# Graph convolutions of a GNN and FFN kernel: the last three or four target tiles summed from gathered rows by rank, the edge table made for 22 target tiles

## The chip, the cores and the metric

The kernel runs on one core of a Trainium2 chip. The metric is the device time of one execution in microseconds, as the median over several runs. The engines are called by the profile's names: PE (TensorE), DVE (VectorE), ACT (ScalarE), POOL (GpSimd) and SP (SyncE, which only issues DMAs). PEld is PE's loading of weights.

## The reference

A graph of 3125 nodes with 256 features and 50000 directed edges, sorted by their target, goes through four pairs of a graph layer and a feed-forward layer, all in FP32. Each adds to `x` and reads a layernorm of it:

```python
x = x + L0_gnn(layernorm(x))    # graph attention, 4 heads
x = x + L0_ffn(layernorm(x))    # 8 experts, top 2
x = x + L1_gnn(layernorm(x))    # two graph attention layers
x = x + L1_ffn(layernorm(x))    # an LSTM over the nodes
x = x + L2_gnn(layernorm(x))    # three graph convolutions
x = x + L2_ffn(layernorm(x))    # 8 experts, top 2
x = x + L3_gnn(layernorm(x))    # one graph convolution
x = x + L3_ffn(layernorm(x))    # 8 experts, top 2
```

What the change touches is the graph convolutions. A layer of the third block is

```python
# src, dst hold the edges and a self loop for each node; norm = disq[src] * disq[dst]
h = h @ W
msg = h[src] * norm[:, None]
h = segment_sum(msg, dst, num_segments=n) + b      # relu between layers
```

with `disq` the inverse square root of a node's number of incoming edges. The fourth block's single layer is the same without self loops and bias.

## The kernel before

**Tiles and stages.** Nodes stand in 25 tiles of 128 (`NT`), the last one with 53 real nodes. `x` stays in SBUF. The stages follow one another: first attention (`gnn0`), experts f0, second and third attention (`gnn1`), the LSTM (`recurrence`: a projection, then rounds), the three convolutions g2 (`gcn`), experts f2, the convolution g3 (`gcn`), experts f3.

**The edge table.** A convolution sums, for each target node, the rows of its sources. The kernel does that as matmuls with a table `ctm` of edge counts, sources by targets, in bf16. `table` (L640) makes it during the first attention in 200 windows of 16 targets: DVE compares keys (L662, L672), PE makes three matmuls for each window (L681), ACT casts them (L688), SP stores them. Between windows, `ahead` (L1224) issues a share of the gathered attention, whose edges POOL fetches by indirect DMA (L2023) and which the later sweep over tiles finishes; `apart.share` rises to 0.55 over the windows.

**Two convolutions, transposed.** `convolve` (L1529) walks over spans of four or three target tiles. For each it loads the table's columns by `table_columns` (L814; five source tiles to a DMA, three buffers) and, over 25 source tiles, makes 2 x 3 matmuls (two halves of the features, three bf16 parts of the FP32 rows `hs`), into `acc0` and `acc1` with two buffers each. `done` scales them on DVE (L1663), applies bias and relu on ACT (L1664), multiplies by the next layer's weights on PE (L369), scales on ACT into `new` (L1656), and `parted` (L840) splits `new` into three bf16 parts, on POOL (casts L847, L849) and DVE (L848, L850). Self loops are an identity that POOL adds to the loaded columns (L828).

**Two convolutions by rows.** `convolve_rows` (L1546), the last layer of g2 and the one of g3, walks over spans of two target tiles with the table as stationary operand (L1560: two parts, 512 wide; L1564: the third, 256 wide); DVE adds the scaled sums to `x` (L1684). After each span, `ready` hands pieces of the expert routing (`experts.front`: norms, router, scatter of rows by L2348) to later steps of the loop, by lags in steps of one target tile and source tile. Weight loads for the experts are spread over the same steps.

**What sets the order.** Each engine runs its own list of instructions in order. The lists come from the order in which the program records instructions and from the scheduler of the framework, which places them by its own estimate of time. `issue_after(ins)` orders only what is on the engine of `ins`. DMA queues take transfers in order of issue: SP for table columns and weights, ACT for stored rows, POOL for gathers and scatters.

**Experts.** `load_ahead` (L2400) loads, once the table's last columns are on the queue, row units (`load_rows`) and first weights (`load_first`, 1158 KB each for f2); f2 has `early=6, ahead=2, more=3`.

**Projection.** In `recurrence` (L1801 to L1824) 98 steps each make 16 matmuls into `px`, four PSUM buffers, which DVE adds to the bias into `pre`.

**Flags.** Numbers in `flags` that are not zero at the end start a second, general computation (L2816 on), which doesn't use the early assumptions.

## Time and profile before

| quantity | value |
|---|---|
| median of 3 runs | 4117.46 us (4089.36 to 4130.27) |
| the profiled execution | 4123.68 us, span 4121.8 us, mean granted TensorE clock 0.913 |
| busy share of the span | PE 86%, PEld 52%, DVE 52%, POOL 34%, ACT 29% |
| table windows (first to last cast) | 94.7 to 437.7 us |
| LSTM projection | 1759.4 to 1826.2 us |
| g2, two transposed convolutions | 2539.1 to 2761.5 and 2761.5 to 2984.0 us |
| g2, convolution by rows | 2984 to about 3200 us |
| f2 experts | about 3240 to 3607 us |
| g3, projection and convolution | about 3607 to 3900 us |
| f3 experts | about 3900 to 4121 us |
| DMA | 422.32 MB, mean 102 GB/s |

The times of stages are from the span's start. A group of instructions in the profile has its line, engine, operation, tiles, count, busy time, mean duration in ns, and the idle time of its engine just before, with what released it. Matmuls overlap: a duration of 379 ns can go with a spacing of 220 ns, so spacings are taken from the timeline. Idle time of an engine that is not the bottleneck costs nothing.

### The profile page before, as it was taken

To read this page: it belongs to the slowest core of one execution; us is meant where nothing else is said; L and a number is where in the kernel's file an instruction comes from. 1 tells how busy PE (TensorE), PEld (TensorE's weight loads), DVE (VectorE), ACT (ScalarE), POOL (GpSimd) and SP (SyncE) were. 2 spreads that over 40 slices of the span, in tenths; PEclk is the share of its full clock that TensorE was granted. 3 is DMA by queue.
4 is the path that set the end of the run, shared out by engine and by line. 5 is a ranking of instruction groups with operands and counts; after the bars stand their busy time and mean duration, and the time that the engine had idled before them with its cause. 6 is when DMAs were issued, how large, how long until landed. Compare 5 with 4: busy or idle time off the path is not lost. (4 is left out here: it accounts for less than half of the span.)

```text
span 4121.8 us, 72442 instructions
## 1 busy us (share of the span) xinstructions
PE 3555.9 (86%) x25990; PEld 2149.1 (52%) x26079; DVE 2155.3 (52%) x7897; ACT 1212.7 (29%) x4041; POOL 1401.9 (34%) x1321
## 2 busy tenths in 40 slices
PE   4567878676878868899999998999999999989988
PEld 3233222463222356675454455555566788856677
DVE  7567788646766645557677675111156411153411
ACT  2455333434333302114444444000100322330122
POOL 2756666444767357400000003111122222222243
PEclk8666887798989979999999999999999999989999
DMA  4444432563333254300000002333364444445465
GB/s 123 136 137 143 141 105 79 142 223 109 107 105 108 73 156 140 87 3 2 2 2 2 2 2 61 88 94 92 91 197 143 144 117 117 122 129 157 134 158 122
DMA packets 366387, 422.32 MB, mean 102 GB/s; under 512 B 44076, under 2 KB 320864, under 8 KB 362295
## 3 DMA queue, kind: packets, MB, share of 16 engines
q1 hardware_dynamic: 286833, 260.46, 21.0%
q0 software_dynamic: 62224, 140.41, 13.1%
q10 hardware_dynamic: 16950, 16.54, 1.2%
q8 instruction: 219, 3.59, 0.4%
q14 instruction: 161, 1.32, 0.1%
HBM read 337.37 MB, written 82.62 MB: 102 GB/s over the span
## 5 line engine op out<-in xcount | busy, mean ns | idle before, releaser
L2023 POOL DMA_INDIRECT edge<-scored,from x720 | 830.6, 1154 | 517.9 <-issue 238.9
L1540 PE MATMUL acc<-c,hs 128*128 128x512 bf16 (+1 forms) x2069 | 405.9, 356 | 1.7 <-POOL hs L847 0.2
L1801 PE MATMUL pz<-lstm_v,hist 128*32 128x192 f32 x7120 | 382.5, 333 | 19.3 <-DVE hist L1906 7.3
L1560 PE MATMUL acc<-hs,c 128*128 128x512 bf16 x1192 | 394.9, 379 | 0.0
L2689 PE MATMUL ph<-xt,first 128*128 128x256 f32 (+1 forms) x1624 | 351.1, 371 | 5.7 <-ACT xt L2655 3.1
L1564 PE MATMUL acc<-hs,c 128*128 128x256 bf16 x1250 | 340.6, 272 | 3.0
L2707 PE MATMUL py<-w,ht 128*128 x1484 | 337.8, 382 | 4.5 <-issue 4.1
L2082 ACT ACTIVATE edge<-edge,factor 128x65 f32<-128x65 f32 (+1 forms) x960 | 251.3, 349 | 218.8 <-DVE factor L2077 170.4
L2689 PEld LDWEIGHTS ph<-xt,first 128*128 128x128 f32 x1624 | 290.6, 196 | 41.3 <-ACT xt L2655 5.4
L1540 PEld LDWEIGHTS <-hs 128*128 128x128 bf16 x2100 | 205.6, 98 | 199.2 <-POOL hs L847 0.6
L2707 PEld LDWEIGHTS py<-w,ht 128*128 128x128 f32 x1484 | 282.9, 192 | 43.6 <-issue 5.2
L976 DVE SCALAR_TENSOR_TENSOR v<-q,g1ahv,c 128x384 f32<-128x384 f32 (+1 forms) x400 | 240.4, 646 | 112.0 <-remote 52.3
L1837 PE MATMUL pz<-pre,ident 128*128 128x192 f32 x900 | 268.4, 381 | 12.1 <-PEq L1914 11.6
L1801 PEld LDWEIGHTS pz<-lstm_v,hist 128*32 128x32 f32 x7120 | 186.0, 109 | 167.7 <-DVE hist L1906 135.9
L2348 POOL DMA_INDIRECT slots<-rows,sloti x150 | 168.5, 1123 | 307.5 <-DVE rstd L345 136.7
L2697 ACT ACTIVATE ht<-ph,first 128x256 f32<-128x256 f32 (+1 forms) x406 | 160.8, 456 | 323.2 <-PE ph L2689 284.3
L681 PE MATMUL pa<-hi,lo 128*128 128x350 bf16 (+2 forms) x600 | 166.4, 422 | 96.8 <-ACT cols L688 40.4
L1611 POOL TENSOR_TENSOR disc<-deg,expo 128x25 f32<-128x25 f32 x1 | 4.4, 4360 | 714.6 <-DVE ends L1911 714.6
L1131 PE MATMUL acc<-g1bhv,v 128*128 128x257 f32 x850 | 218.0, 407 | 25.2 <-issue 9.9
L1884 ACT ACTIVATE z<-pz 128x128 f32<-128x128 f32 (+1 forms) x900 | 176.5, 248 | 198.1 <-PE pz L1801 197.5
L2092 PE MATMUL edgeacc<-edge,hot 128*32 128x264 f32 (+1 forms) x1440 | 152.3, 468 | 82.2 <-issue 35.1
L1837 PEld LDWEIGHTS pz<-pre,ident 128*128 128x128 f32 x900 | 136.0, 190 | 149.0 <-issue 70.3
(530 smaller groups left out, 5499.2 us busy)
## 6 DMA issues: line engine op xcount, KB each, us to landing
c<-ct SPq DMA_DIRECT2D x103, 640.0 KB
c<-ct SPq DMA_DIRECT2D x75, 480.0 KB
first<-in_f_first SPq DMA_DIRECT2D x29, 1158.0 KB
slots<-slots SPq DMA_DIRECT2D x159, 130.0 KB
ct<-cols SPq DMA_DIRECT2D x12, 1600.0 KB
first<-in_f_first SPq DMA_DIRECT2D x29, 642.0 KB
edge<-scored,from POOLq DMA_INDIRECT x720
first<-in_f_first SPq DMA_DIRECT2D x29, 385.0 KB
```

The source lines that it names most:

```text
L976: nc.vector.scalar_tensor_tensor(to, q[:, h, :w], hv[:, s, h, D // nh + 1 : D // nh + 2], cols[s], op0=ALU.max, op1=ALU.mult,)
L1131: nc.tensor.matmul(a[:, : D + 1], v[0][:, j * P : (j + 1) * P], hv[:, s, 0, : D + 1], start=(s == 0), stop=(s == NT - 1),)
L1540: self.nc.tensor.matmul(acc[f][:, : n * P], lhs, cols[s], start=(s == 0 and i == 0), stop=(s == NT - 1), skip_group_check=True,)
L1560: nc.tensor.matmul(acc[t], lhs, hs[:, s, 0:2, :].rearrange("p i d -> p (i d)"), start=start, stop=stop, skip_group_check=True,)
L1564: return nc.tensor.matmul(acc[t][:, D:], lhs, hs[:, s, 2, :], start=False, stop=stop, skip_group_check=True,)
L1801: made = nc.tensor.matmul(pz[q * R : (q + 1) * R, :], s, m, start=start, stop=stop, tile_position=(0, q * R),)
L1837: made = nc.tensor.matmul(pz, self.ident, pre[:, g, s, :], start=True, stop=False)
L1884: nc.scalar.activation(three[0][:, gates, :], three[1][:, gates, :], AF.Tanh)
L2023: nc.gpsimd.indirect_dma_start(out=tile[:, g, :], out_offset=None, in_=self.rows, in_offset=bass.IndirectOffsetOnAxis(ap=index, axis=0),)
L2082: nc.scalar.mul(part, part, factor[:, g, h : h + 1])
L2689: made = nc.tensor.matmul(ph[:, m - m0, :n, :], st["w1"][:, k * hid + m * P : k * hid + (m + 1) * P], st["xt"][:, k, :n, :], start=(k == 0 ...
L2707: nc.tensor.matmul(py[:, j, :], st["ht"][:, m, j, :], st["w2"][:, m * D : (m + 1) * D], start=(m == 0), stop=(m == nhc - 1),)
```

## The change

**Near tiles.** With `NEAR = 4`, `RANKS = 22` and `FAR = NT - NEAR = 21`, the last four target tiles (21 to 24) of the transposed convolutions, and the last three (22 to 24) of those by rows, get no matmuls with the table. `NearTiles` sums their sources by rank instead: the r-th incoming edge of each of 128 targets is fetched as one indirect gather of 128 rows from a DRAM copy of the layer's rows (`sources`, written by `put_rows` on ACT's queue), two gathers to a buffer `got`, five buffers; DVE adds them, 128x512 at a time. Edges beyond rank 22 are fetched by one more gather (`more`, at most 128 rows) and spread by a matmul with `beyond_hot`. The end of a near tile is one or two further adds, the scale, and in the transposed layers two transposes, relu and the next product. The recording goes by a clock of 0.325 us for each target tile and source tile.

**The plan.** `near_plan`, 15 pieces recorded after every fourth step of the LSTM projection, works out the indices: degrees, offsets by prefix sums (`before`, two matmuls and a scan on DVE), four gathers of windows of the sorted edges (`win`), five shifts by binary digits (`shifted`, three DVE instructions each), the ranks, the leftovers and one gather of their pairs. Two flags are added: more than 128 leftovers, and a rank whose target doesn't fit.

**The rest.** The table is made for 22 tiles of targets, 176 windows; the gathered attention's share beside it is 0.52. Spans of the transposed convolutions are 4, 3, 4, 3, 4, 3 tiles instead of 4, 4, 3, 4, 3, 4, 3, those of the rows eleven of two instead of twelve and one of one. The routing of the near tiles is taken up after targets 12 and 18. The weights of `gcn` stand in a pool that ends before the rows; in g3 their load comes ahead of the loads of `x` on SP's queue. Experts that store load four row units ahead (f2 two before), f2 one first weight ahead (two before), and `run` loads all early row units at its start into a pool of their own.

```diff
+NEAR, RANKS = 4, 22
+FAR = NT - NEAR
...
+        self.sources = [dram.tile([NP + P, D], F32, name=f"sources{i}") for i in range(2)]
...
+        def where():
+            before(indeg, NT, off)
+            nc.vector.tensor_copy(at, off)
+            nc.vector.tensor_scalar(
+                row, at, RUN.bit_length() - 1, None, op0=ALU.logical_shift_right
+            )
+            for i in range(NEAR):
+                nc.gpsimd.indirect_dma_start(
+                    out=win[:, i, :], out_offset=None, in_=self.runs,
+                    in_offset=bass.IndirectOffsetOnAxis(ap=row[:, i : i + 1], axis=0),
+                )
...
+        def shifted(j):
+            step = 2 << j
+            upto_ = size + step - 2
+            now = pairs[:, :, :upto_]
+            nc.vector.tensor_sub(less[:, :, :upto_], pairs[:, :, step : step + upto_], now)
...
+            nc.vector.tensor_add(now, now, less[:, :, :upto_])
...
-        block, end = 2 * P // WIN, NT * P // WIN
+        block, end = 2 * P // WIN, (FAR + 1) * P // WIN
...
-                        apart.share = 0.55 * (i + 1) / len(windows)
+                        apart.share = 0.52 * (i + 1) / len(windows)
...
-        for t0, n in even_spans(wide):
+        for t0, n in even_spans(wide, FAR if near else NT):
...
-                        self.nc.tensor.matmul(
+                        made = self.nc.tensor.matmul(
...
+                if near:
+                    near.upto(n, made.ins)
...
-        for t0, n in spans(wide):
+        for t0, n in even_spans(wide, near.first if near else NT):
...
+            for other in fronts.pop(t0 + n, ()) if near else ():
+                for lag, piece in ready(*other):
+                    waiting.append((step + 24 + lag, piece))
...
+                def end():
+                    self.put_rows(self.sources[layer % 2], new, t0, n)
+                    self.parted(lefts, to, new, t0, n)
...
+                def near_done(t, rows, i=i, after=after, next_layer=next_layer):
+                    turned, agg = [], aggs.tile([P, KD, P], F32, name="nearagg")
+                    def turn():
+                        pt = psum.tile([P, KD, P], F32, name="tp", padded_shape=[P, 512 // P, P])
+                        for f in range(KD):
+                            nc.tensor.transpose(
+                                pt[:, f, :], rows[:, f * P : (f + 1) * P], self.ident
+                            )
+                        for f in range(KD):
+                            nc.scalar.activation(
+                                agg[:, f, :], pt[:, f, :], AF.Relu, bias=bs[i][:, f : f + 1]
+                            )
+                    def use():
+                        new, end = rows_of(after, t, 1, i + 1)
+                        next_layer(t, agg, new[:, 0, :])
+                        end()
+                        if i == 0:
+                            nc.vector.tensor_add(x[:, t, :], x[:, t, :], bias)
+                    return [turn, use]
...
+                if split and t0 + n == FAR - 1:
+                    lags = [2] + [22 + 4 * j for j in range(n)] + [34, 40, 46]
...
-                if t0 + n == CERTAIN:
-                    lags[-1] += 32
+                if experts.sent == CERTAIN:
+                    lags[-1] += 20 if split else 32
...
+            rest = self.convolve_rows(
+                cpool, accp, loops, hs, add, ready, loads,
+                near_tiles(len(weights) - 1, FAR + 1, 3.9, near_add),
+                {12: [(FAR + 1, 2)], 18: [(FAR + 3, 1)]},
...
+                pieces = self.near_plan(inner) if turned else []
...
+                        if pieces and s % 4 == 3:
+                            pieces.pop(0)()
...
+class NearTiles:
+    def __init__(self, net, pool, gots, psum, rows, hs, disc, first, pace, done):
+        self.net, self.nc, self.gots, self.psum = net, net.nc, gots, psum
+        self.rows, self.hs, self.disc, self.first, self.done = rows, hs, disc, first, done
+        self.pool, self.got, self.now, self.adding = pool, [], 0.0, done.__name__ == "near_add"
+        self.tiles = range(first, NT)
+        self.each = RANKS // 2
+        self.waiting, t0 = [], 5.0
+        self.more = pool.tile([P, D], F32, name="more")
+        self.put(t0, lambda: self.gather(self.more, self.net.beyond))
+        for i, t in enumerate(self.tiles):
+            state, begin = {}, t0 + i * self.each * pace
+            self.put(begin + 9.0, lambda t=t, state=state: self.begin(t, state))
+            for b in range(self.each):
+                at = begin + b * pace
+                self.put(at, self.fetch)
+                self.put(at + 9.0, lambda t=t, b=b, state=state: self.add(t, b, state))
+            self.put(at + 9.1, lambda t=t, state=state: self.end(t, state))
+    def put(self, at, piece):
+        self.waiting.append((at, piece))
+        self.waiting.sort(key=lambda entry: entry[0])
+    def gather(self, to, index):
+        with self.net.tc.issue_after(self.last):
+            self.nc.gpsimd.indirect_dma_start(
+                out=to, out_offset=None, in_=self.rows,
+                in_offset=bass.IndirectOffsetOnAxis(ap=index, axis=0),
+            )
+    def fetch(self):
+        n = len(self.got)
+        t, b = self.first + n // self.each, n % self.each
+        got = self.gots.tile([P, 2, D], F32, name="got")
+        for j in range(2):
+            r = 2 * b + j
+            self.gather(got[:, j, :], self.net.ranked[:, t - FAR, r : r + 1])
+        self.got.append(got)
+    def upto(self, n, last=None):
+        if n is None:
+            while self.waiting:
+                self.waiting.pop(0)[1]()
+            return
+        self.now, self.last = self.now + 0.325 * n, last
+        while self.waiting and self.waiting[0][0] <= self.now:
+            self.waiting.pop(0)[1]()
+    def begin(self, t, state):
+        nc, x, by = self.nc, self.net.x, self.disc[:, t : t + 1]
+        pm = self.psum.tile([P, 512], F32, name="tp")
+        nc.tensor.matmul(
+            pm[:, :D], self.net.beyond_hot[:, t - FAR, :], self.more, start=True, stop=True
+        )
+        base = state["base"] = self.pool.tile([P, D], F32, name="base")
+        if self.hs is None:
+            nc.vector.tensor_copy(base, pm[:, :D])
+        else:
+            nc.vector.tensor_add(base, pm[:, :D], self.hs[:, t, 0, :])
+            for i in range(1, PARTS):
+                nc.vector.tensor_add(base, base, self.hs[:, t, i, :])
+        state["sums"] = self.pool.tile([P, 2, D], F32, name="sums")
+    def add(self, t, b, state):
+        n = (t - self.first) * self.each + b
+        if b == 0:
+            return
+        sums = state["sums"]
+        self.nc.vector.tensor_add(sums, self.got[n - 1] if b == 1 else sums, self.got[n])
+    def end(self, t, state):
+        nc, x, base, sums = self.nc, self.net.x[:, t, :], state["base"], state["sums"]
+        by = self.disc[:, t : t + 1]
+        nc.vector.tensor_add(base, base, sums[:, 0, :])
+        nc.vector.tensor_add(base, base, sums[:, 1, :])
+        if self.adding:
+            nc.vector.scalar_tensor_tensor(x, base, by, x, op0=ALU.mult, op1=ALU.add)
+        else:
+            nc.vector.tensor_scalar(base, base, by, None, op0=ALU.mult)
+        for i, piece in enumerate(self.done(t, base)):
+            self.put(self.now + 3.0 * (i + 1), piece)
-            for i in range(max(self.ahead, self.rows)):
+            for i in range(4 if self.store else self.rows):
...
+            if self.early and self.store:
+                self.slot_rows = net.pool(inner, self.name + "later", self.early)
+                for i in range(self.early):
+                    if i not in self.state:
+                        self.load_rows(i)
...
-            store=True, early=6, ahead=2, more=3,
+            store=True, early=6, ahead=1, more=3,
```

## The prediction

> **What bounds the kernel now.** I read the busy time by stretch first, because the change acts in four stages with different limits; then the timeline of the engines that the change loads, and last the waits of single lines. The first view gives, for each stretch, its length and the busy time of each engine, then the granted TensorE clock, the DMA share and GB/s.
>
> ```profile
> core 0: us, PE busy (x) PEld busy (x) DVE busy (x) ACT busy (x) POOL busy (x), PEclk, DMA share, GB/s
> 86.50:437.70 351.20, 229.04 (x1625) 109.56 (x1625) 229.21 (x488) 176.31 (x539) 224.93 (x190) 0.64 0.49 143
> ...
> 1759.40:1826.20 66.80, 66.26 (x1569) 61.46 (x1569) 36.40 (x107) 0.00 (x1) 0.21 (x1) 0.96 0.01 3
> 2539.10:2761.50 222.40, 221.54 (x1119) 119.55 (x1133) 27.62 (x42) 20.09 (x41) 26.03 (x52) 1.00 0.32 93
> 2761.50:2984.00 222.50, 221.67 (x1123) 118.68 (x1135) 27.56 (x41) 17.87 (x35) 26.55 (x51) 1.00 0.31 90
> 2984.00:3200.00 216.00, 214.34 (x1362) 137.43 (x1389) 128.87 (x818) 12.80 (x37) 50.73 (x66) 1.00 0.54 166
> ```
>
> The last three rows are the two transposed convolutions and the three-part row convolution. PE is busy for over 99% of each at full clock, while VectorE and GpSimd have most of their time free. So a matmul left out there is time gained, unless PE is made to wait. In the first row (table windows beside gathered attention) no engine is full and the clock is 0.64: a chain, not an engine, sets its pace. The second row is the LSTM projection: PE-bound, with VectorE half free.
>
> How PE goes through the first convolution, with start and length:
>
> ```profile
> 2539.11 28.87 PE L1540 MATMUL acc<-c,hs 128*128 128x512 bf16 x131
> 2568.07 3.72 PE L369 MATMUL tp<-L_gnn_W,agg 128*128 128x256 f32 x16
> 2571.63 32.65 PE L1540 MATMUL acc<-c,hs 128*128 128x512 bf16 x149
> 2604.25 3.72 PE L369 MATMUL tp<-L_gnn_W,agg 128*128 128x256 f32 x16
> ```
>
> One span of four targets is 32.65 us, hence 32.65/(4 x 25) = 0.3265 us for a target tile and source tile; with the three-target span (24.43 us) 0.325, or **8.13 us for a target tile**. The product follows 2 us into the next span, and it needs the evacuation on VectorE (`agg`, 1.29 us for two). This evacuation is the spot to watch: PE has 2 us of other work before it must have come.
>
> A gather of 128 rows on GpSimd, back to back, in an attention stage:
>
> ```profile
> 1068.68 0.95 POOL L2023 DMA_INDIRECT edge<-scored,from  x1 [0.30 <-issue]
> 1069.93 0.94 POOL L2023 DMA_INDIRECT edge<-scored,from  x1 [0.30 <-issue]
> 1071.18 0.94 POOL L2023 DMA_INDIRECT edge<-scored,from  x1 [0.30 <-issue]
> ```
>
> One starts every **1.25 us** (0.95 busy and 0.30 of issue). And what GpSimd already does in the convolutions: it adds the identity of the self loops to the table's chunk (L828), waiting for each load of it.
>
> ```profile
> L828 POOL TENSOR_TENSOR c<-c,ident x75: 420/427/954, 2484.9 to 3202.0; 128x128 bf16<-128x128 bf16 x75
> ...
>   DMA c<-ct: 209.9, 24
> ```
>
> **The matmuls removed.** Two transposed convolutions lose four target tiles each, two row convolutions three each: 8 x 8.13 + 6 x 8.13 = 65 + 49 = **-114 us**. The row convolutions do the same pairs as 512- and 256-wide matmuls, 602 pairs in the 216 us stretch that also holds expert routing, so 0.325 holds there as well. What comes back on PE: for each of 14 near tiles a matmul for the edges beyond rank 22, and in the transposed layers two transposes and smaller products, at 0.22 us a 256-wide matmul; about 0.9 us x 8 + 0.25 x 6 = **+9**. On VectorE ten 128x512 adds a tile at 0.69 us (row L848), some 7 us a tile against 195 us free in a layer: hidden. The 34 or so extra stores of the product to DRAM are issued by ACT (20 us busy of 222), and the DMA share is 0.3 to 0.5: nothing.
>
> **The gathers, and what stands behind them.** A transposed layer adds 1 + 88, a row layer 1 + 66: 312 gathers. At 1.25 us a layer's gathers need 111 us of a 222 us layer, so the total fits. But the changed program as built doesn't spread them: the pace written in the code sets the order in which things are recorded, no gather waits for a matmul, and on GpSimd's queue they come in a bunch at each layer's start. What is queued behind them decides:
>
> Layer one: on VectorE ten adds of the first near tile and nine of the second stand before the first span's evacuation. They need 42 gathers, after the one for the leftovers; GpSimd can start at 2541.3, when its last casts are through, and has three identity adds between (0.43 us each). 2541.3 + 43 x 1.25 + 1.3 = 2596.4. Landing: the software queue's 62224 packets took 13.1% of 16 engines' span, 0.139 us each, so 8 packets an engine are 1.1 us, an estimate from the page; then an add (0.7) and evacuation with relu (1.5): the product can start at about 2599.7. PE wants it at 2568 + 2 (it has nine matmuls ahead of it). Stall **30 us**.
>
> Layer two: gathers start when the last rows are stored and GpSimd's casts are done, 7 us in (2990.90 against 2984 at the next boundary). 20 adds, 44 gathers + 1: 7 + 56.3 + 1.3 + 1.1 + 2.2 = 68 against 33 + 2 wanted. Stall **32**.
>
> Layer three (rows, g2): here the matmuls themselves wait for the identity adds. Behind 13 gathers the second span's pair is done at 7 + 16.3 + 0.8 = 24, wanted at 17.6: 6.5. Behind 32 more the third span's is at 65, wanted at 35.1 + 6.5 = 41.6: 23. Stall **30** together. Later spans have one bunch of 10 to 12 each, inside 16.3 us.
>
> Layer four (g3) has no identity adds, and its evacuations stand between the adds, with a second accumulator as slack: **0**, but the scatter of normed rows to the experts comes after 54 gathers (68 us), which 130 us of span still cover.
>
> So of 114 us the stalls give back 92 and PE's extra work 9: **-13** in the convolutions. Bounds: gathers without the 0.30 issue gap (0.95 us, its lower row) make the three stalls 133 x 0.30 = 40 us shorter; the whole trace's pace of L2023, busy 830.6 and idle 517.9 over 720, 1.87 us, makes them 82 longer. I take 1.25, since VectorE and DMA are quiet here as there.
>
> There is a rule that speaks against this. The Trainium skill, SBUF — State Buffer, section SBUF: two separate sides, says that GpSimd and a VectorE instruction with two SBUF inputs (against GpSimd work that reads SBUF) lock each other out of a shared port for a whole instruction, and that descriptors of GpSimd's DMAs then come late. Every pair of gathers has one 0.69 us add beside it; by the rule each gather would cost up to 0.35 us more, and the sum would be 133 x 0.35 = 46 us higher. The trace speaks for the other side: in the table stage, with VectorE 65% busy, the median of 178 gathers is 949 ns, the quiet figure.
>
> **The table.** 176 windows of 16 targets instead of 200. The windows' casts (L688, x200) run from 94.7 to 437.7: 343/200 = 1.72 us a window, 24 windows are 41 us if everything in the stretch shrinks in step. The other bound is TensorE's part alone, 24 x 3 x 0.277 = 20 us (L681, 165.1 us for 596), and less what the lower share moves: 0.52 for 0.55 leaves some 12 more gathers' matmuls and adds to the later sweep, 0.3 to 0.6 us each, 4 to 8. Range -12 to -41; I take **-27**.
>
> **The plan of ranks.** Some 80 small VectorE instructions (0.16 to 0.7 us) enter the projection, which has 30 us of VectorE free, but the first dozen `pre` adds (0.358 us) have plan work before them and PE holds only four buffers of 0.68 us: **+6**, from +1 (all in the gaps) to +17 (all of it in line). Four window gathers, 5 us, are beside it on an idle GpSimd.
>
> **Experts and weights.** More row units loaded ahead: PE waits 4.17 us for slots at 3258, 7.67 and 3.29 at 3925; of these 15 I take **-8**. Against it one 1158 KB weight load of f2 now comes after the convolution: at the q1 rate in the row stage about 5 us, so -15 to +5. g3's W load goes ahead of the x loads on SP's queue, a wait of 4.06 us at 3622: **-4**, or 0 if x is what is late.
>
> **Sum.** -13 - 27 + 6 - 8 - 4 = -46. Against the profiled execution's 4123.7 (span 4121.8 and 1.9 around it) that is 4077.7; it lies 6.2 above the median of the runs shown, so in those terms **4071 us**, 1.1% faster. A measurement of this kernel can tell about 1%, which is 41 us.
>
> **Rivals.** (1) *The gathers don't hold PE*: they run faster than one in 0.95 us, or evacuations pass. Then the stalls, 92, fall by 40 or more: 4031 down to 3979; I take 4000. For it: PE has nothing else to wait for. Against: queues are served in order, and no row shows under 0.94. (2) *Slower*: in one place, GpSimd's queue at the start of layers one to three, a gather takes 1.87 us as L2023 does over the trace. 133 gathers stand before the three points, so the price is 133 us for each us: the gain is gone from 1.25 + 46/133 = 1.60, and over 1% is lost from 1.91. At 1.87: 4071 + 82 = 4153. For it: the gather's mean is 1154 ns, and DMA is half full in layer three. Against: nearly all of that excess is idle time before other work. (3) *No change*: the table stage is paced by its gathers and not by windows (-12), and the expert loads only move (+5): 4071 + 15 + 13 = 4099. (4) *It doesn't do what it says*: over 128 leftover edges, or a wrong rank, sets a flag and the general path runs; no row prices that, and I put it beyond 4155. The degrees of 50000 random edges on 3125 nodes, 16 on average, leave few beyond 22.
>
> **How the numbers follow.** Forecast 0.43 (0.27 of it over 1% faster), rival one 0.20, three 0.13, two 0.22 (0.16 of it over 1% slower), four 0.02. That makes faster 0.47, same 0.35, slower 0.18. The likeliest case's own range, from its terms, is 4030 to 4115; to leave out no more than 2 in 10, half of rival one and the upper part of rival two are let in: 3990 to 4155.
>
> **What would show it.** Right: PE idle of about 30 us early in each of the first three layers, ended by VectorE's evacuation in two and by GpSimd's identity adds in the third; layers of about 222 - 32 + 33; a table stretch some 30 us shorter; g3's rows 20 us shorter. Wrong: layers of 190 us with PE still 99% busy (rival one), gathers in the bunch further apart than 1.6 us (rival two), a table stretch as long as before (rival three).

## The result and the profile after

The changed kernel takes 4239.25 us (median of six runs, 4236.93 to 4257.64) against 4117.35 for the kernel before in the same comparison: a ratio of 1.0319, interval 1.0285 to 1.0353. It is 3.2% slower; 4071 us and 1.1% faster were forecast. The profiled execution took 4236.93 us. The head of its page, to set against 86%, 52%, 34% and a clock of 0.913 before (0.891 now):

```profile
span 4235.2 us, 72054 instructions
PE 3482.6 (82%) x25393; PEld 2102.7 (50%) x25473; DVE 2261.1 (53%) x8154; ACT 1207.2 (29%) x4030; POOL 1727.7 (41%) x1640
```

PE did less work and the span became longer, so the loss is idle time. Its place is read from the busy times by stretch. The rows answer to the table stage, the LSTM projection, the two transposed convolutions and g2's convolution by rows; the last row is g3's convolution:

```profile
core 0: us, PE busy (x) PEld busy (x) DVE busy (x) ACT busy (x) POOL busy (x), PEclk, DMA share, GB/s
86.10:403.20 317.10, 210.32 (x1533) 100.99 (x1537) 211.59 (x462) 161.43 (x502) 226.46 (x180) 0.65 0.49 144
1748.20:1815.20 67.00, 67.00 (x1570) 62.94 (x1573) 41.67 (x141) 0.59 (x1) 0.95 (x1) 0.97 0.02 5
2530.60:2773.80 243.20, 199.73 (x994) 111.04 (x1004) 65.69 (x109) 24.15 (x51) 114.85 (x144) 0.89 0.43 131
2773.80:3022.30 248.50, 208.50 (x1007) 113.08 (x1017) 65.14 (x108) 21.51 (x45) 113.30 (x140) 0.90 0.43 130
3022.30:3305.00 282.70, 220.02 (x1278) 135.02 (x1303) 159.34 (x936) 13.29 (x40) 117.64 (x133) 0.87 0.51 154
...
3726.70:4016.00 289.30, 230.34 (x1373) 146.90 (x1400) 136.73 (x630) 30.17 (x77) 121.17 (x136) 0.89 0.48 145
```

g3's convolution before:

```profile
3655.60:3879.40 223.80, 220.90 (x1410) 141.26 (x1437) 97.71 (x543) 9.32 (x25) 43.22 (x48) 1.00 0.50 146
```

Before, PE filled about 99% of each layer of 222 to 226 us. Now 40 to 63 us of each layer are idle and the granted clock is 0.87 to 0.90 where it was 1.00. By stage, in us, from first to last instruction of the stage (layer one counts from its first table matmul, among the products ahead of it):

| stage | before | after | change |
|---|---|---|---|
| table windows and the attention sweep after them | 649.4 | 639.5 | -9.9 |
| layer one | 257.8 | 282.1 | +24.3 |
| layer two | 226.1 | 248.5 | +22.4 |
| g2 rows | 225.5 | 282.7 | +57.2 |
| g3, from the last matmul of f2 | 276.8 | 313.4 | +36.6 |
| all others | | | -17 |

So the four convolutions, forecast at -13, are at +140. Two things are seen in layer one's timeline of PE (start, length, engine, line, tiles; the idle time before it and what ended it):

```profile
2576.61 0.59 PE L1734 MATMUL acc<-c,hs 128*128 128x512 bf16 x1 [2.91 <-issue]
2578.71 0.59 PE L1734 MATMUL acc<-c,hs 128*128 128x512 bf16 x1 [1.51 <-issue]
...
2606.61 5.16 PE L373 MATMUL tp<-L_gnn_W,agg 128*128 128x256 f32 x16 [6.83 <-ACT agg L1905]
```

The product waits for the evacuation, as forecast, and comes 76 us after the start of the stretch at 2530.6. But the wait itself is only 7 us, because PE arrives late: from 2557 to 2596 it gets single matmuls, mostly 2 to 3 us apart, while GpSimd gathers without a break. The runs below fall into two kinds by the chip they ran on. On one, as here, the kernel before takes about 4110 us (one chip of the runs below, and the chip of this comparison); on the other about 3940 (three chips), and there PE keeps its full rate beside the gathers, and the forecast stall stands alone.

### The profile page after: what moved, and what is told of

It reads as the page before. It is cut to its first block, busy times and chain, and to the rows that moved or that the text cites. A ratio compares the mean times of both kernels' runs of the same rounds, so it can differ in the third digit from the quotient of the medians.

```text
span 4235.2 us, 72054 instructions
## 1 busy us (share of the span) xinstructions
PE 3482.6 (82%) x25393; PEld 2102.7 (50%) x25473; DVE 2261.1 (53%) x8154; ACT 1207.2 (29%) x4030; POOL 1727.7 (41%) x1640
## 5 line engine op out<-in xcount | busy, mean ns | idle before, releaser
L1734 PE MATMUL acc<-c,hs 128*128 128x384 bf16 (+1 forms) x1774 | 360.1, 358 | 61.0 <-issue 59.3
L1758 PE MATMUL acc<-hs,c 128*128 128x512 bf16 x1046 | 366.9, 394 | 38.4 <-issue 31.4
L2393 POOL DMA_INDIRECT got<-sources,ranked x308 | 303.3, 985 | 175.8 <-DVE sums L2436 81.5
L1762 PE MATMUL acc<-hs,c 128*128 128x256 bf16 x1100 | 308.7, 281 | 38.1 <-issue 35.2
L1734 PEld LDWEIGHTS <-hs 128*128 128x128 bf16 x1800 | 177.3, 99 | 235.5 <-issue 77.8
L2691 POOL DMA_INDIRECT slots<-rows,sloti x150 | 179.6, 1197 | 239.8 <-DVE rstd L349 58.4
```

What stands on the lines that cost most here:

```text
L1734: made = self.nc.tensor.matmul(acc[f][:, : n * P], lhs, cols[s], start=(s == 0 and i == 0), stop=(s == NT - 1), skip_group_check=True,)
L1758: nc.tensor.matmul(acc[t], lhs, hs[:, s, 0:2, :].rearrange("p i d -> p (i d)"), start=start, stop=stop, skip_group_check=True,)
L1762: return nc.tensor.matmul(acc[t][:, D:], lhs, hs[:, s, 2, :], start=False, stop=stop, skip_group_check=True,)
L2393: self.nc.gpsimd.indirect_dma_start(out=to, out_offset=None, in_=self.rows, in_offset=bass.IndirectOffsetOnAxis(ap=index, axis=0),)
```

## The experiments

Theory A is queue order: what PE needs stands on VectorE or GpSimd behind instructions that wait for gathers. Its first rival is that the gathers by themselves slow PE.

**Spare gathers in the kernel before** (all on a chip where it takes 3938 us). At the start of g3's rows, 54 gathers that nothing reads are put on GpSimd's queue:

```diff
+                for g in range(54):
+                    got = gots.tile([P, 256], F32, name="spared")
+                    with self.tc.issue_after(made.ins):
+                        made = nc.gpsimd.indirect_dma_start(
+                            out=got[:128], out_offset=None, in_=rows,
+                            in_offset=bass.IndirectOffsetOnAxis(ap=idx[:128], axis=0),
+                        )
```

> The kernel before, with 54 spare gathers of 128 rows of 1 KB (from the input x, into buffers that nobody reads) in one unbroken run on GpSimd's queue at the start of g3's row convolution, where no matmul needs anything from GpSimd. Before, the first to the last matmul of that layer take 223 us. Theory 'unbroken run' (after some 15 gathers in a row without a gap, every other engine gets about one instruction for each gather): the first 15 are free, the other 39 cost PE nearly all of 39 x 1.25 us, so the layer takes 265 to 275 us, with PE at about 8 matmuls and weight loads together in 10 us. Rival 'queue order' (PE was late only through what stands behind the gathers on GpSimd and VectorE): nobody waits for these gathers, the layer stays at 223 to 228 us.

3977.93 us; the rows took 255.3 us, 32 more than without spares. PE ran at full rate beside 37 gathers and then stopped until they were through. So here unbroken gathers did not slow it; work behind them did. What stands behind them can be read off: a scatter of routed rows comes next on GpSimd, VectorE's copy into a buffer of rows waits for it, and PE's routing matmul waits for VectorE's top-2 selection (`sel`) behind that copy:

```profile
3558.49 0.58 PE L2282 MATMUL tp<-sel,after 128*128 128x16 f32 x2 [29.91 <-DVE sel L2273]
```

```profile
3555.97 0.17 DVE L2236 COPY rows<-rows 128x2 f32<-128x2 f32 x1 [41.33 <-DMA slots<-rows,sloti]
```

With three GpSimd memsets of 128x1024 after every ninth gather:

```diff
+                    if g % 9 == 9 - 1:
+                        for _ in range(3):
+                            with self.tc.issue_after(made.ins):
+                                made = nc.gpsimd.memset(still, 0.0)
```

> The same 54 spare gathers, but after every ninth GpSimd fills a 128x1024 buffer three times, some microseconds without a gather. 'Unbroken run': no run reaches 15, PE keeps its rate, the layer takes 223 to 230 us. 'It is the number of gathers, or their traffic': as in the unbroken run, 265 us or more. 'Queue order': 223 to 228 us, as in the unbroken run.

3994.82 us, rows 272.3: the pauses made it longer, as time in the queue does. The 18 memsets take 17.3 us, and the copy's wait grew from 41.3 to 58.4 us.

With 64 rows to a gather, and with rows of 256 bytes (the second pair of lines):

```diff
-                            out=got[:128], out_offset=None, in_=rows,
+                            out=got[:64], out_offset=None, in_=rows,
...
-                rows = self.w["x"].rearrange("n (a b) -> (n a) b", b=256)
+                rows = self.w["x"].rearrange("n (a b) -> (n a) b", b=64)
```

> 54 spare gathers in one run, each of 64 rows instead of 128. If what fills up is counted in rows (descriptors), PE slows only after some 30 gathers, and loses 24 x 1.25 = 30 us at most (less if a gather of 64 rows starts sooner); the layer takes 240 to 255 us. If it is counted in gathers, PE slows after 15 and loses as much as in the full run for the time that the run then lasts. 'Queue order': 223 to 228 us.

> 54 spare gathers in one run, each of 128 rows of 256 bytes instead of 1 KB. If the bytes moved (DMA share, writes into SBUF) slow PE, the loss falls to a quarter or less: the layer takes 223 to 240 us. If it is the issuing of gathers, it is as in the full run: 265 to 275 us.

3973.12 and 3989.23 us, rows 253.6 and 255.3. Neither half the rows nor a quarter of the bytes brought it down: a gather starts every 1.22 to 1.26 us in all three, so the number of instructions on GpSimd sets it.

**The changed kernel again, paced, and without gathers.** First on the other kind of chip, unedited:

> The changed kernel once more. In the profiled run of the change, PE got about one instruction for each gather from the 15th gather of an unbroken run on; with the spare gathers on the kernel before, in a job where that kernel took 3938 us instead of 4117, PE kept its full rate beside 37 gathers and then stopped for what stood behind them. If the one-instruction-for-each-gather state belongs to the chip (or to the day) and this job's kernel before takes about 3940 us: no such stretch, only the stalls by queue order of the prediction (30 us in each of three layers), and the change at -20 to -60 us. If this job's kernel before takes about 4117 us: +110 to +130 us as in the first comparison.

4062.66 us, ratio 1.0312 (1.0295 to 1.0329). Layers 274.7, 239.0, 272.0 and 284.0 us. PE, and VectorE just before, in layer one:

```profile
2430.51 6.16 PE L373 MATMUL tp<-L_gnn_W,agg 128*128 128x256 f32 x16 [35.39 <-ACT agg L1905]
```

```profile
2422.46 0.69 DVE L2436 TENSOR_TENSOR sums<-sums,got 128x512 f32<-128x512 f32 x1 [1.81 <-DMA got<-sources,ranked]
2424.98 0.72 DVE L2436 TENSOR_TENSOR sums<-sums,got 128x512 f32<-128x512 f32 x1 [1.83 <-DMA got<-sources,ranked]
2428.40 0.69 DVE L2436 TENSOR_TENSOR sums<-sums,got 128x512 f32<-128x512 f32 x1 [2.71 <-DMA got<-sources,ranked]
2429.01 1.28 DVE L1904 TENSOR_TENSOR agg<-acc,dis 128x512 f32<-128x512 f32 x2
```

The evacuation stands directly behind the last of the adds, each of which waits for its gathers. Layer two has the same stall, 32.83 us.

Next, gathers made to wait for a newly landed chunk of table columns:

```diff
-                    near.upto(n, made.ins)
+                    near.upto(n, made.ins, cols[s][:, 0:1] if s % GRP == 0 else None)
...
+        if chunk is not None:
+            self.mark = self.nc.gpsimd.tensor_copy(self.marked, chunk).ins
```

> The changed kernel, with the gathers really paced: at every fifth source tile GpSimd copies one column of the table's chunk that has just landed, and the gathers recorded after that stand behind the copy on GpSimd's queue. Chunks land as PE frees buffers, so the gathers follow PE. On VectorE the first span's evacuation now stands behind 9 adds (20 gathers) instead of 19 (42). Theory 'queue order': the stalls of 30 us in the first three layers go nearly away, 60 to 90 us less than the changed kernel in the same job, whatever the chip. Theory 'unbroken runs': runs are at most 15 long and then 4, so the slow stretches go too; together some 100 to 180 us less where those stretches occur. Rival 'the number of gathers costs': within 20 us of the changed kernel.

3994.99 us, ratio 1.0145 (1.0124 to 1.0166): layers 259.9, 221.0, 258.4, 267.3. Over half of the loss goes by spreading the same gathers.

Then no gather of rows at all; the near tiles get sums of zeros:

```diff
     def gather(self, to, index):
+        self.nc.vector.memset(to, 0.0)
+        return
```

> The changed kernel without the 312 gathers of rows: the sums of the near tiles add one buffer of zeros instead, so what the near tiles yield is left out, while adds, products, table and plan stay. All that the gathers cost is then gone: each transposed layer takes 222 - 32.5 + 3.5 = 193 to 198 us, each row layer 24 us less than before. If a layer stays above 210 us, what slows it isn't the gathers.

3875.6 us: layers 229.5, 199.3, 220.8, 230.5. Against the unedited run the gathers cost 45, 40, 51 and 47 us (g3 with what lies ahead of it: 54 us less in the rows, which start 7 later). Without them the change would be 1.7% faster (one run). But the row layers gained little even so: g2's rows are 4.6 us shorter than the 225.4 of a kernel with the table for all tiles, where three tiles' matmuls were to bring 24.

Last, the loads of experts and weights alone in the kernel before:

```diff
+            early = self.pool(inner, name + "weights", 1)
...
-            for i in range(max(self.ahead, self.rows)):
+            for i in range(4 if self.store else self.rows):
...
-            store=True, early=6, ahead=2, more=3,
+            store=True, early=6, ahead=1, more=3,
```

> The kernel before with only the experts' and weights' part of the change (four row units ahead, one first weight of f2 instead of two, the other row units at the start of the run, the weights' pool). Predicted as -8 - 4 us. In the first comparison, from the end of g3's rows to the last expert matmul of f3 took 199.7 us instead of 223.4, and from f2's last to g3's first row matmul 24 instead of 53. If this part brings that, the kernel is 20 to 50 us faster than before in the same job; if those gains are work that the longer layers hid, it stays within 12 us.

3931.03 us, one run, against a median of 3941.34 (3935.86 to 3944.9): -10.3.

**One cause at a time** (a chip where the kernel before takes 4109 us). Adds may not be placed ahead of the evacuation recorded before them:

```diff
+        sums, after = state["sums"], getattr(self.net, "scaled", None)
+        with self.net.tc.issue_after(after) if after else nullcontext():
+            self.nc.vector.tensor_add(sums, self.got[n - 1] if b == 1 else sums, self.got[n])
```

> The changed kernel with one edit: an add of gathered rows that is recorded after the evacuation of a span may not be placed ahead of it on VectorE. Theory A (VectorE's order alone holds PE in layers one and two): the stalls of 35 and 33 us that end with VectorE's evacuation go, layer one falls from 275 to about 240 us and layer two from 239 to about 206, the row layers stay at 272 and 284; in all about 65 us less than the changed kernel on the same chip. Theory B (GpSimd's queue holds PE as well: the identity adds for the second span's table columns stand behind the same gathers and were through 7 and 25 us after PE would want them): the stall is only renamed, it ends with GpSimd's identity add, and each layer gains 5 to 15 us.

4209.82 us. Layer one 248.8, layer two 215.2: 33.3 less in each. PE reaches the same product without a wait:

```profile
2594.94 3.62 PE L373 MATMUL tp<-L_gnn_W,agg 128*128 128x256 f32 x16
```

Theory A holds: VectorE's order alone made these stalls. The first version under "The row layers" below has the same edit in these two layers, on the other kind of chip: 233 and 199 us there, against 230 and 199 with no gather at all. The rows (282.2, 289.8) did not move.

The table for all 25 tiles again:

```diff
-        block, end = 2 * P // WIN, (FAR + 1) * P // WIN
+        block, end = 2 * P // WIN, NT * P // WIN
```

> The changed kernel with the table made for all 25 target tiles again (200 windows, share of attention 0.55), near tiles as they are. Theory A (the smaller table brings nothing: what leaves the windows comes back in the sweep): the windows take 283 us for 272, the sweep after them 278 to 280 for 297, so the stretch is 3 to 7 us shorter than in the changed kernel on the same chip, and so is the run. Theory B (the prediction's term): the run is 20 to 27 us longer. The convolutions are as in the changed kernel either way: 275, 239, 272 and 284 us.

4261.85 us, one run, inconclusive as a whole: windows and sweep took 647.7 us, with the small table 639.5 (after) and 647.3 (the pinned version), with the large one 649.4, 644.6 and 640.7. On the other kind of chip it took 567.4 us in the mean of eight profiles with the small table (565.6 to 569.9) and 562.6 in six with the large one (560.8 to 566.8). So the smaller table brings nothing that can be seen on one and costs some 5 us on the other.

Near tiles in the transposed convolutions alone, the table for all tiles:

```diff
-        for t0, n in even_spans(wide, near.first if near else NT):
+        for t0, n in spans(wide):
...
-                near_tiles(len(weights) - 1, FAR + 1, 3.9, near_add),
-                {12: [(FAR + 1, 2)], 18: [(FAR + 3, 1)]},
+                None, {},
```

> The changed kernel with near tiles in the two transposed convolutions alone; both convolutions by rows use the table for all tiles, as before the change, and the table has 200 windows. Theory A (in the row layers the gathers cost more than the matmuls they replace, through the routing pieces and identity adds queued behind them): g2's rows fall from 272 to about 225 us and g3's from 284 to about 223 with 50 us instead of 24 ahead of them; layers one and two stay at 275 and 239; in all 65 to 80 us less than the changed kernel on the same chip, so still over the kernel before by 40 to 55. Theory B (the row layers' loss is the f2 and f3 routing and weights part, which stays): they stay within 15 us of 272 and 284.

4158.57 us. g2's rows 225.2, g3 267.5 from the last matmul of f2 (before 276.8). Near tiles were a loss of 57 and 46 us in the row layers. Theory A's sum is met within a us (81 less than the changed kernel in the first comparison), though g3's rows alone took 243 us, not 223, with 24 us ahead of them, not 50.

The same with the three edits shown for pacing, pin and expert loads:

> The kernel before with near tiles in the two transposed convolutions alone, each pair of gathers made to wait for a newly landed chunk of table columns (a copy of one column on GpSimd), the adds kept behind the evacuation recorded before them on VectorE, the table for all tiles, and the changed kernel's loads for the experts. Theory A (queue order is the whole cost, and four near tiles are worth their matmuls once it is gone): layer one 232 to 245 us, layer two 202 to 215, rows as before at 225 and 223, experts 10 us less; in all 20 to 55 us less than the kernel before on the same chip, a ratio of 0.986 to 0.995. Theory B (the gathers and their adds cost PE time even when spread, through identity adds that come late for every span): layers one and two stay over 250 and 218, and the run is within 1% of the kernel before or longer.

4078.18 us, ratio 0.9916 (0.9884 to 0.9947): 0.8% faster than the kernel before, a small gain of which the loads, at -10.3 where they ran alone, make a part, and the best of those that leave nothing out. Its three layers of g2:

```profile
2529.00:2730.50 201.50, 191.81 (x975) 106.37 (x984) 63.20 (x106) 22.69 (x48) 122.67 (x170) 0.97 0.53 155
2730.50:2936.20 205.70, 198.17 (x1007) 108.86 (x1017) 65.50 (x109) 21.35 (x45) 123.29 (x169) 0.99 0.53 158
2936.20:3161.60 225.40, 223.61 (x1422) 143.37 (x1450) 138.11 (x886) 13.66 (x40) 51.70 (x67) 1.00 0.56 168
```

In the first two rows stand the same gathers and adds as in the rows of after above, and some 27 small copies on GpSimd more: 243 and 248 us have become 201 and 206, and the clock is back. The third row has no near tiles.

**The row layers** (chips where the kernel before takes 3942 us). The pinned version without the row layers' adds (near tiles there get sums of zeros):

```diff
+            if self.adding:
+                if b == 1:
+                    self.nc.vector.memset(sums, 0.0)
+                return
```

> The kernel with pinned evacuations (layers of 249, 215, 282 and 290 us where it was run), and in the two convolutions by rows the adds of gathered rows on VectorE left out (the gathers stay, the near tiles get sums of zeros). Theory A (in the row layers the routing chain on VectorE, and so TensorE's routing matmuls, stand behind adds that wait for gathers): g2's rows fall to 235 to 250 us, g3's to 235 to 255. Theory B (GpSimd's queue or the unbroken gathers themselves hold TensorE): both stay above 265.

3959.7 us; rows 268.6 and 268.2, against 272.0 and 284.0 in the unedited run: theory B's numbers. Leaving out the adds brought little. Yet in the unedited run adds do stand in the chain. PE's longest wait in g2 there, and VectorE's list before it:

```profile
2896.81 0.66 PE L356 MATMUL tp<-ident,plain 128*128 128x128 f32 x2 [17.50 <-DVE plain L2541]
```

```profile
2892.15 0.69 DVE L2436 TENSOR_TENSOR sums<-sums,got 128x512 f32<-128x512 f32 x1 [1.74 <-DMA got<-sources,ranked]
...
2894.67 0.69 DVE L2436 TENSOR_TENSOR sums<-sums,got 128x512 f32<-128x512 f32 x1 [1.76 <-DMA got<-sources,ranked]
...
2896.25 0.73 DVE L2541 TENSOR_SCALAR plain<-x,mv,rstd 128x256 f32<-128x256 f32 x2
```

The norms of the routing stand between adds that each wait for gathers; in g3 the same chain held PE for 14.2 and 12.8 us. With the adds gone, another chain of about the same length takes its place. PE's longest wait in g3 without the adds, what stands ahead of it on VectorE, and the end of the gathers on GpSimd:

```profile
3570.97 0.58 PE L2612 MATMUL tp<-sel,after 128*128 128x16 f32 x2 [37.08 <-DVE sel L2603]
```

```profile
3568.39 0.17 DVE L2566 COPY rows<-rows 128x2 f32<-128x2 f32 x1 [48.50 <-DMA slots<-rows,sloti]
3568.48 0.16 DVE L2590 TENSOR_TENSOR logits<-tp,L_ffn_bg 128x16 f32<-128x16 f32 x1
...
3570.67 0.16 DVE L2603 TENSOR_SCALAR sel<-sel 128x16 f32<-128x16 f32 x1
```

```profile
3560.48 0.95 POOL L2395 DMA_INDIRECT got<-sources,ranked  x1 [0.30 <-issue]
3561.73 1.00 POOL L2698 DMA_INDIRECT slots<-rows,sloti  x1 [0.30 <-issue]
```

It is the chain of the spare gathers, with four links. The scatter of a routed span stands behind the gathers on GpSimd; VectorE's copy into one of three buffers of rows waits for that scatter; the top-2 selection stands behind the copy; PE's position matmul (`sel`), and all matmuls after it, wait for the selection. In g2 7.0 and 23.7 us end with GpSimd's identity adds. Before the change the same copy waited 5.8 to 7.2 us in g3 and 3.5 to 4.1 in g2, and PE never stood still for it.

The edits for pacing and pin together, in all layers:

> The changed kernel with both cures in every layer: adds kept behind the evacuation recorded before them, and gathers behind a GpSimd copy of a column of each newly landed table chunk. Theory A (VectorE's order holds the row layers): layers one and two as in the version with near tiles there alone (241 and 206 us, or 15 less on a chip where the kernel before takes 3940), but rows still at 255 to 265 and 265 to 275, because adds still wait for gathers ahead of the routing chain. Theory B (unbroken gathers hold them): rows at 225 to 240 and 235 to 250.

3936.86 against 3942.19 us: layers 234.6, 198.0, 257.9, 266.2. The transposed layers gain 24 and 28 us on before; the row layers lose them again.

The row layers' adds on GpSimd in place of VectorE:

```diff
+            to = self.nc.gpsimd if self.adding else self.nc.vector
+            to.tensor_add(sums, self.got[n - 1] if b == 1 else sums, self.got[n])
```

> The paced and pinned version, with the adds of gathered rows in the two convolutions by rows issued on GpSimd in place of VectorE, so that no instruction of VectorE waits for a gather there. Theory A (VectorE's order): g2's rows 225 to 240 us, g3's 225 to 245, in all 20 to 50 us less than the paced and pinned version with VectorE's adds and a ratio to the kernel before of 0.985 to 1.0. Theory B (GpSimd's time): 66 gathers at 1.25 us and 30 adds of over 0.7 us make some 110 us on GpSimd, its identity adds and scatters come later still, and rows stay at 255 or more.

3972.62 us, ratio 1.0074 (1.0052 to 1.0095), rows 272.2 and 276.0: theory B, and one more sign that time on GpSimd is what counts.

The spare gathers once more:

> The kernel before with 54 spare gathers unbroken at the start of g3's rows, once more. If the chip is of the kind where the kernel before takes 4110 us: the theory that unbroken gathers slow TensorE by themselves expects full rate for some 15 gathers and then about one matmul per gather, and g3's rows at 280 us or more; the theory that only queue order counts expects full rate for 37 gathers, then a stop, and 255 us. If the chip is of the other kind, 255 us by either.

3975.93 us, rows 255.2, on the kind of chip where PE keeps its rate beside gathers: it repeats the first run and tells nothing new.

Deeper buffers of rows, without the row layers' adds and, in the second run, with all cures and the row layers' adds recorded 15 us after their gathers in place of 9:

```diff
-        self.sends = self.net.pool(ctx, self.name + "frontrows", 3)
+        self.sends = self.net.pool(ctx, self.name + "frontrows", {"f2": 4, "f3": 8}.get(self.name[:2], 3))
```

> The version that leaves out the row layers' adds of gathered rows, with more buffers for the rows that are scattered to the experts: eight in place of three in g3, four in g2 (no more fit). Theory A (the scatters stand behind the gathers on GpSimd, VectorE waits for them to refill a buffer, and TensorE's routing matmuls wait for VectorE): the 37 us stall of g3 goes, its rows fall from 268 to 225 to 238 us; g2 changes by less than 12 us, since one more buffer is 16 us of slack and its 24 us stall is GpSimd's identity add. Theory B (the copy only happens to wait; other work in GpSimd's queue or the gathers themselves hold TensorE): g3's rows stay over 255.

3964.1 us, g3's rows 265.0 (270.7 with a wait of 5.6 us ahead of the first matmul). The copy waits as long as before, and PE 38.75 us behind it:

```profile
3575.13 0.21 DVE L2566 COPY rows<-rows 128x2 f32<-128x2 f32 x1 [50.09 <-DMA slots<-rows,sloti]
```

By its number this is theory B, but the chain is still theory A's. VectorE's instruction list shows why: the copy reads a constant only, and it seems that the scheduler places it as soon as its own estimate has a buffer free. With three buffers the first three copies stand at the layer's start and the fourth ahead of the second selection; with eight, the first eight stand at the start and the ninth in that very place. The buffers moved copies, not the wait.

> The paced and pinned version with near tiles in all four convolutions, with the deeper row buffers (eight in g3, four in g2) and the row layers' adds recorded 15 us after their gathers in place of 9. Theory A (scatters and adds in queues are what is left): g3's rows fall from 266 to 230 to 245 us, g2's from 258 to 240 to 252, in all 25 to 50 us less than the paced and pinned version and a ratio to the kernel before of 0.986 to 0.993. Theory B: rows within 8 us of 258 and 266, ratio 0.997 to 1.002.

3952.69 us, ratio 1.003 (1.002 to 1.0039), rows 258.2 and 261.5 (267.1 with the wait ahead): theory B's numbers. Whether the copy, bound to its own span, would free the row layers wasn't tried; since one chain has taken the place of another here, it is not shown.

## Why the prediction was wrong

**Right, in mechanism and size: the stalls of layers one and two.** 30 and 32 us were forecast from VectorE's order and a gather each 1.25 us. They measured 35.4 and 32.8 where nothing else disturbed them, and keeping VectorE's order took 33.3 us out of each on the other chip. (Layer two's terms add up to 33, not 32.) The gathers kept the pace (0.95 busy, 0.30 of issue, unbroken).

**Right in layers one and two: the matmuls.** With the stalls gone, layer two fell from 226.1 to 198.0, -28.1; the steps gave -32.5 for four tiles and +3.6 for PE's extra work. The plan of ranks, +6 forecast, cost 1.4 in the projection; the loads of experts and weights, forecast at -12, were -10.3 in one run.

**Wrong, and most of the miss: the row layers.** By the two profiles the run came out 159 us above the sum: 115 in the row layers (forecast +6 and, with g3's weights, -28; measured +57 and +37), 43 in layers one and two, 17 in the table, less 15 in all other stages. Two steps failed there.

The first is "**0**, but the scatter of normed rows to the experts comes after 54 gathers (68 us), which 130 us of span still cover". It gave the evacuations slack and asked when the experts need the scatter. It left out the routing: norms and selection stand on VectorE between the adds, and PE's routing matmuls wait for them (17.5 and 9.9 us in g2, 14.2 and 12.8 in g3). And it did not ask who waits for the scatter itself: VectorE, for a buffer, after three spans, with PE 37 us behind it once the adds are gone. For g2 the step had 6.5 and 23 us for the identity adds and left out the routing as well: in the unedited run the first wait was 7.1 us, and in the second's place PE waited for the norms; the 23.7 came up without the adds. In place of 30 and 0 the gathers cost 51 and 47. That the gathers are the cause is shown, by the run without them and by the spare ones; no edit of a single chain freed these layers.

The second is the saving of the matmuls, -24 in each row layer. Without any gather g2's rows came out 4.6 us shorter, and g3, from the last matmul of f2, 6 us shorter than with the table for all tiles (261.3 against 267.5, on the two kinds of chip). In g2 PE's busy time fell by 16.8 us, not 24, and it idled some 12 us, with the longest waits (4.1 us twice) for VectorE's selection. Why was not tried, so this part stays open.

**Wrong: what a stall takes with it.** The sum counted waits alone. After the stall of 35 us the 16 matmuls of the product took 6.16 us against 3.72 before, at a granted clock of 0.60, a second stall of 5 us followed in each layer, and on the chip of the recorded times PE lost 15 to 16 us a layer beside unbroken gathers: pinned 248.8 and 215.2 us, against 233 and 199 for the same edit on the other kind. Pacing took back 7.7 and 9.5 of it (241.1 and 205.7).

**Wrong: the table, -27.** It was -9.9 in one pair of profiles, inside their scatter, and about +5 on the other kind of chip. The windows did shrink (343.0 to 308.9 us), but the sweep after them grew from 306.4 to 330.6. The step priced what moves to the sweep at 4 to 8 us; 24 came back.

**The rivals.** The first (gathers don't hold PE) is refuted by the stall lines. The second asked for gathers at 1.87 us and named the right place, GpSimd's queue at a layer's start; the loss came at 1.25 us, through waits that it did not count, so its direction was right by luck. The rule of the Trainium skill that the prediction weighed (SBUF — State Buffer, section SBUF: two separate sides) would, by the prediction's estimate, have slowed each gather beside a two-input add by up to 0.35 us. The 308 gathers of the profile after averaged 0.985 us, with a median of 0.949, the figure that the prediction called quiet: so it was right to leave it out.

## What to carry to other kernels

Before work is put at the head of an in-order queue, list everything else on that queue, and for each item everyone who waits for it, down to the one who only wants its buffer back; a send that "nobody needs yet" still holds a buffer that a busy engine will ask for. Work that is spread in the order of recording isn't spread on the chip unless it waits for something that comes at that pace. More buffers do not help where a scheduler moves the refill forward by as many. And where several chains hang on one queue, taking one away shows the next: in g3 waits of 14.2 and 12.8 us behind the adds gave way to one of 37 behind the scatter. What the queue costs in all is told only by a run without its load.

## What was not expected of the hardware

On the chips where the kernel before takes about 4110 us, PE got about one instruction for each gather (weight loads counted) once some 15 gathers had followed one another without a break. These rows are two stretches of layer one in the profile after, with GpSimd's gathers (and two or so other instructions) in the last of the busy columns:

```profile
2557.00:2575.00 18.00, 4.32 (x9) 0.81 (x8) 5.66 (x9) 0.00 (x0) 13.83 (x15) 0.63 0.35 102
2575.00:2596.00 21.00, 4.11 (x7) 0.93 (x9) 4.85 (x7) 0.00 (x0) 12.88 (x14) 0.50 0.30 87
```

Sixteen matmuls and 17 weight loads beside 27 gathers in 39 us, where some 180 matmuls fit at the kernel before's 32.65/150 us each. The idle times end with "issue", so with nothing that the profile shows. On the chips of 3940 us PE kept its full rate beside 37 spare gathers. The kernel before shows the difference too, and only where it gathers: up to the LSTM projection, with 720 gathers of edges in the attention stages, it took 1759 us on one kind and 1577 on the other, and from there to the first table matmul of g2 740 on both. The ratio of the changed kernel to the one before is about the same on both kinds (1.0319 and 1.0312). That is in part chance: its four convolutions are 7, 10, 11 and 5 us longer on the slower kind, and the table's stretch is 9.9 us shorter than before there and some 5 longer on the other. The cause was not found: the repeat of the spare gathers fell on the other kind of chip.
